# All attention exponentials through the DMA transpose: one transpose path instead of two, with three score buffers

## The chip, the cores and the metric

The kernel runs on one core of one Trainium2 chip. The metric is the device time of one execution in microseconds (us), the median of several runs. Five engines work side by side, each through its own queue in order: TensorE (PE; its weight loads are shown apart as PEld), VectorE (DVE), ScalarE (ACT), GpSimd (POOL) and SyncE (SP), which here only issues DMAs.

## The reference

The input x has 4 batches of 1024 tokens with 256 features. Four residual layers follow one another, each on a layer norm of x: a linear recurrence (LRU) with a small MLP, a gated feed-forward with two top-32 selections per token (FFN), an attention, and the same FFN again. The change touches the attention alone, but the attention runs beside parts of both FFNs.

```python
q = (x @ Wq.T).reshape(b, t, N_HEADS, HEAD_DIM)          # 8 heads of 64
kv_latent = x @ Wkv_down.T                               # 64 wide, shared by the heads
k = (kv_latent @ Wk_up.T).reshape(b, t, N_HEADS, HEAD_DIM)
v = (kv_latent @ Wv_up.T).reshape(b, t, N_HEADS, HEAD_DIM)
scores = jnp.einsum('bqhd,bkhd->bhqk', q, k) * scale
attn = jax.nn.softmax(scores, axis=-1)                   # no mask: 1024 keys for each query
out = jnp.einsum('bhqk,bkhd->bqhd', attn, v)
return out.reshape(b, t, N_HEADS * HEAD_DIM) @ Wo.T
```

Wk_up is folded into the queries and Wv_up into the output weights, so that keys and values of all heads are the same 64-wide latent rows. kh and kl are its two parts with the tokens along the free axis; la (float32), or lb0 and lb1 (float16 high and low part), are the same rows with tokens on the partitions.

## The kernel before

The work is in stages. The LRU and the first layer norm of the FFN come first; then the first FFN's tiles of batch 0 with the attention's preparation; then, with pools of their own, the attention of all four batches; then the rest of the second FFN. The middle stage is the one that changes. In it heads() runs for each batch b over 2 blocks of 512 queries (nb), 4 pairs of heads (g) and 4 tiles of 128 queries (q): 32 iterations a batch, 128 in all. An iteration treats two heads (j = 0, 1), called halves here: 256 halves in all. A half is a chain over the engines: PE multiplies queries by keys into a PSUM tile sc of 128x1024 (line 877), DVE takes the negated maximum of each row (nm, 881), ACT takes the exponential into pr and sums the rows (885). For the product with the values the exponentials must lie with the keys on the partitions, so they are transposed. There are two ways, and by_dma picks by the parity of q:

- q even: ACT casts pr to float16 (888), POOL forms the remainder as a second float16 (889), both into pd; SP issues one DMA that transposes all of it into d0 or d1 (890). DVE has added 11 ln 2 to the maximum's negative before (883), so that the small parts stay in range. The values are then summed over 24 terms per half, in float16 (values_sum, line 921).
- q odd: PE transposes pr itself, eight blocks per half into PSUM tiles ptp of four (896); ACT copies them out to p0 or p1 (901; in the last batch DVE copies every first one, 899). The values are summed over 8 terms per half, in float32.

values_sum also takes the reciprocal of the row sums (rs, 915), spreads it on POOL (rows, 917), lets PE transpose that (929), copies it (rb, ACT, 931) and multiplies (on, DVE, 932). It is called late: for an odd q in the next iteration's first half, for an even q in the second half of the next even iteration, so that the DMA has time to land.

merge() weaves side work into the halves at fixed places: the queries of the next group (queries, 849), the output product of a finished query block (output, 942 and 944), the second FFN's layer norm and first product on finished tokens (head), the next batch's keys (prepare, values), and for b < 3 the eight FFN tiles of the next batch (tile: two top-32 selections on DVE at line 670, with POOL, ACT and PE parts; it starts at half 12 + 4i of 64). The order that results on each engine is then set by a scheduler with a timeline of its own; each engine follows that order.

PSUM has eight banks. In this stage two score buffers take four ("sc": 2), the transposes two ("t": 2) and all else shares two ("s": 2). In SBUF, d0 and d1 have two buffers each, pd two, pr three, rows two, xg (the tile's gated input, line 651) two.

Of the kernel before, what the change touches and what calls it, by code (L numbers as in the profile page):

```python
# [10 lines left out]
F32 = mybir.dt.float32  # L11
# [3 lines left out]
F16 = mybir.dt.float16  # L15
AF = mybir.ActivationFunctionType
ALU = mybir.AluOpType
AX = mybir.AxisListType
PSUM = bass.MemoryType.PSUM
DRAM = bass.MemoryType.DRAM  # L20

P = 128
B = 4
T = 1024
D = 256
KD = D // P
TPB = T // P
# [3 lines left out]
HD = 64  # L31
# [455 lines left out]
class Ffn:  # L487
# [100 lines left out]
    def tile(self, i, sp, psum, tags, out=None, fast=False, parts=None, tt=None):  # L588

        nc, w = self.nc, self.w  # L590
# [14 lines left out]
        nm = sp.tile([P, 2], F32, tag="nm", name="nm")  # L605
        ssum = sp.tile([P, 2], F32, tag="ssum", name="ssum")
# [11 lines left out]
        for r in range(nr):  # L618
            for s in range(2 if r else 0):
                self.ordered(nc.vector.max, m8[:, s, r, :], wk[:, s, :])  # L620
            for s in range(2):
                v, k = (wk, m8[:, s, r, :]) if r else (ex, e8[:, s, :])
# [6 lines left out]
        q = i % 4  # L629
# [17 lines left out]
            pool.tensor_tensor(ob, ob, ex[:, 0, :], ALU.mult)  # L647
        yield

        xg = sp.tile([P, D], F32, tag="xg", name="xg", bufs=2)  # L650
        sc = sp.tile([P, 2], F32, tag="sc", name="sc")
        pool.tensor_scalar(sc, norm[:, :, q], rs[:, 1:2], 0.0, ALU.mult, ALU.add)
        nc.scalar.activation(xg, x, AF.Identity, bias=sc[:, 1:2], scale=sc[:, 0:1])
# [112 lines left out]
PSHIFT = 11  # L766


class Attention:
# [8 lines left out]
    def prepare(self, b, nb, psum, tag, groups=((0, 1), (2, 3)), whole=True):  # L778


        nc, sp, wp = self.nc, self.sp, self.wp
        xs = self.x[b * TPB + 4 * nb : b * TPB + 4 * nb + 4]
        xnt = self.xnt[b, nb] = [
            wp.tile([P, KD, 512], F32R, tag=f"xnt{nb}{part}", name=f"xnt{nb}{part}") for part in range(2)
        ]
        if nb == 0:
            self.k[b] = (
                wp.tile([P, T], F32R, tag="kh", name="kh", bufs=2),
                wp.tile([P, T], F32R, tag="kl", name="kl", bufs=2),
                wp.tile([P, TPB, HD], F32, tag="la", name="la", bufs=2),  # L790
                [wp.tile([P, TPB, HD], F16, tag=f"lb{i}", name=f"lb{i}", bufs=2) for i in range(2)],
            )
        if whole:
            scales = layer_norm(nc, sp, "ax4", xs)
            yield
        for group in groups:
            views = [xs[q] for q in group]
            if whole:
                rstd, shift = (t[:, group[0] : group[-1] + 1] for t in scales)
            else:  # L800
                rstd, shift = layer_norm(nc, sp, f"ax{len(group)}", views)
                yield
            pt = normalized_t(nc, sp, psum, "fx", tag, views, rstd, shift, self.ident)
            sl = slice(group[0] * P, (group[-1] + 1) * P)
            split(nc, *(t[:, :, sl] for t in xnt), pt)
            if not whole:
                self.latents(b, nb, sl, psum, tag)
            yield
        if whole:
            self.latents(b, nb, slice(0, 512), psum, tag)  # L810
            yield
# [11 lines left out]

    def values(self, b, nb, psum, tag):

        nc, (kh, kl, la, lb) = self.nc, self.k[b]
        pv = psum.tile([P, 4, HD], tag, "pv")
        for q in range(4):
            tk = slice((4 * nb + q) * P, (4 * nb + q + 1) * P)
            for i, v in enumerate((kh, kl)):  # L830
                nc.tensor.matmul(pv[:, q, :], v[0:HD, tk], self.sident, start=(i == 0), stop=(i == 1))
        sl = slice(4 * nb, 4 * nb + 4)
        nc.scalar.copy(la[:, sl, :], pv)
        nc.gpsimd.tensor_copy(lb[0][:, sl, :], la[:, sl, :])
        nc.gpsimd.tensor_tensor(lb[1][:, sl, :], la[:, sl, :], lb[0][:, sl, :], ALU.subtract)
        yield

    def queries(self, b, nb, g, psum, tag):
# [13 lines left out]
    def heads(self, b, psum):  # L852

        nc, sp, wp = self.nc, self.sp, self.hp
        kh, kl, la, lb = self.k[b]
        late, pending = [], []
        for nb, g, q in ((nb, g, q) for nb in range(2) for g in range(PAIRS) for q in range(4)):
            by_dma = q % 2 == 0  # L860
            if g == 0:
                self.on[b, nb, q] = wp.tile([P, PAIRS, P], F32, tag=f"on{q}", name=f"on{q}")
            qs = self.qs[b, nb, g]
            ssum = sp.tile([P, 2], F32, tag="ssum", name="ssum", bufs=4)
            if by_dma:
                pts = [wp.tile([P, 2 * TPB, P], F16, tag=f"d{j}", name=f"d{j}", bufs=2) for j in range(2)]
                parts = ((0, lb[0]), (TPB, lb[0]), (0, lb[1]))
                terms = [(v[:, c, :], i + c) for c in range(TPB) for i, v in parts]
            else:
                pts = [wp.tile([P, TPB, P], F32, tag=f"p{j}", name=f"p{j}") for j in range(2)]  # L870
                terms = [(la[:, c, :], c) for c in range(TPB)]
            for j in range(2):
                sc = psum.tile([P, T], "sc", "sc")
                for i, kk in enumerate((kh, kl)):
                    for kb in range(2):
                        sl = slice(kb * 512, (kb + 1) * 512)
                        nc.tensor.matmul(  # L877
                            sc[:, sl], qs[:, j, q * P : (q + 1) * P], kk[:, sl], start=(i == 0), stop=(i == 1)
                        )
                nm = sp.tile([P, 1], F32, tag="nm", name="nm", bufs=4)  # L880
                nc.vector.tensor_reduce(nm, sc, AX.X, ALU.max, negate=True)  # L881
                if by_dma:
                    nc.vector.tensor_scalar(nm, nm, PSHIFT * math.log(2.0), None, ALU.add)  # L883
                pr = wp.tile([P, T], F32, tag="pr", name="pr", bufs=3)
                nc.scalar.activation(pr, sc, AF.Exp, bias=nm, accum_out=ssum[:, j : j + 1])  # L885
                if by_dma:
                    pd = wp.tile([P, 2, T], F16, tag="pd", name="pd", bufs=2)
                    nc.scalar.copy(pd[:, 0, :], pr)  # L888
                    nc.gpsimd.tensor_tensor(pd[:, 1, :], pr, pd[:, 0, :], ALU.subtract)  # L889
                    nc.sync.dma_start_transpose(pts[j], pd.rearrange("p i k -> p (i k)"))  # L890
                else:
                    for half in range(2):
                        pt = psum.tile([P, 4, P], "t", "ptp")
                        for kk in range(4):
                            kc = 4 * half + kk
                            nc.tensor.transpose(pt[:, kk, :], pr[:, kc * P : (kc + 1) * P], self.ident)  # L896
                        dst = pts[j][:, 4 * half : 4 * half + 4, :]
                        if half == 0 and b == B - 1:
                            nc.vector.tensor_copy(dst, pt)
                        else:  # L900
                            nc.scalar.copy(dst, pt)  # L901
                if j == 0 and pending:
                    self.values_sum(*pending.pop(0), psum)
                if j == 1 and late and by_dma:
                    self.values_sum(*late.pop(0), psum)
                yield
            (late if by_dma else pending).append((pts, terms, ssum, self.on[b, nb, q][:, g, :]))
        for args in late + pending:
            self.values_sum(*args, psum)

    def values_sum(self, pts, terms, ssum, on, psum):

        nc, sp = self.nc, self.sp
        rs = sp.tile([P, 2], F32, tag="rs", name="rs")
        nc.vector.reciprocal(rs, ssum)
        rows = sp.tile([P, 2, HD], F32, tag="rows", name="rows")
        nc.gpsimd.tensor_copy(rows, rs[:, :, None].to_broadcast([P, 2, HD]))  # L917
        po = psum.tile([P, 2, P], "s", "pmo")
        for n, (v, c) in enumerate(terms):
            for j in range(2):  # L920
                nc.tensor.matmul(  # L921
                    po[j * HD : (j + 1) * HD, 0, :],
                    v,
                    pts[j][:, c, :],
                    start=(n == 0),
                    stop=(n == len(terms) - 1),
                )

        nc.tensor.transpose(po[:, 1, :], rows.rearrange("p j d -> p (j d)"), self.ident)  # L929
        rb = sp.tile([P, P], F32, tag="rb", name="rb", bufs=1)  # L930
        nc.scalar.copy(rb, po[:, 1, :])  # L931
        nc.vector.tensor_tensor(on, po[:, 0, :], rb, ALU.mult)  # L932
# [92 lines left out]
def tile_kernel(ctx: ExitStack, tc: tile.TileContext, x_in, w_lru, vecs_in, rows, w_ffn, lin_t, w_attn, w_down, out):  # L1025
    nc = tc.nc
# [33 lines left out]
    with ExitStack() as c1:  # L1060
# [16 lines left out]
        for k in range(NBLK):  # L1077
# [11 lines left out]
            b = k // CH + 1  # L1089
# [10 lines left out]
        k = NBLK - 1  # L1100
# [13 lines left out]
    with ExitStack() as c2:  # L1114
# [8 lines left out]
        with ExitStack() as c4:  # L1123
# [8 lines left out]
            with tc.issue_after(f1.gelu(1)):  # L1132
                for blk in range(2, NBLK):
                    g = f1.gelu(blk)
# [26 lines left out]
                    next(aheads, None)  # L1161
            run(second)
            f1.keep, f1.last_topk = False, None
        psum = Banks(c2.enter_context(tc.tile_pool(name="ps2", space=PSUM)), {"sc": 2, "t": 2, "s": 2})
        at.hp = c2.enter_context(tc.tile_pool(name="at_h", bufs=1))
        fp = c2.enter_context(tc.tile_pool(name="f_s", bufs=2))
        for b in range(B):
# [130 lines left out]
```

## Time and profile before

| | us |
|---|---|
| median of 3 runs | 1562.88 |
| lowest and highest | 1562.34, 1567.57 |
| the profiled execution, its own time | 1561.58 |
| its span in the trace | 1559.9 |
| of that, up to the first scores of the attention | 376.7 |
| the attention stage, 376.7 to 1335 | 958.3 |
| what follows | 224.9 |

The profile shows one execution. Busy time of an engine is the time in which it works on an instruction; a wait is idle time in front of an instruction, with the instruction that ended it. Times of POOL are rough, and ends of matmuls are modelled. In the tables of stretches each row gives, for each engine, busy microseconds and in brackets the instructions; then the granted PE clock (1.00 is full), the mean share of the 16 DMA engines that was busy (a share over 1 means that packets stood one behind the other), and GB/s.

### The profile page before, as it was taken

The numbers are of one execution on the slowest core, as the hardware profiler recorded it, in microseconds if no ns is written. First come the engines' busy times: TensorE is split into PE (matmuls) and PEld (weight loads), VectorE is DVE, ScalarE is ACT, GpSimd is POOL, SyncE is SP. The second block draws the span as 40 slices with busy tenths as digits, with TensorE's granted clock in tenths as the row PEclk, the third lists the DMA queues.
The fourth block names the chain that finished last, engine by engine and source line by source line (L and its number), as shares of the span: only waits on it lengthen the run. The fifth ranks groups of instructions, "written<-read, shape, count | busy, mean of one in ns | idle before, by whom it ended". The sixth has DMA issues, their size and how long they took to land.

```text
span 1559.9 us, 28683 instructions
## 1 busy us (share of the span) xinstructions
PE 1303.3 (84%) x10136; PEld 955.5 (61%) x10136; DVE 1193.4 (77%) x3674; ACT 1014.4 (65%) x2145; POOL 681.7 (44%) x848
## 2 busy tenths in 40 slices
PE   5879999697898789988879988879989998667776
PEld 3535556375766667756657866657777776444544
DVE  8977675696599966778976568986675665499998
ACT  5253434654787668777677877767875875476664
POOL 2043423161365533536543435643443533157876
PEclk9989999698999999999999999999999999779888
DMA  3110000331544334453334443414443545000000
GB/s 116 35 36 14 28 14 17 130 122 34 82 79 89 58 62 82 82 86 68 59 61 83 82 72 75 85 35 82 83 82 56 99 79 82 14 11 28 21 24 28
DMA packets 288609, 96.51 MB, mean 62 GB/s; under 512 B 268233, under 2 KB 284626, under 8 KB 288466
## 3 DMA queue, kind: packets, MB, share of 16 engines
q1 hardware_dynamic: 283024, 88.50, 29.3%
q10 hardware_dynamic: 5442, 6.18, 1.2%
q8 instruction: 80, 1.31, 0.3%
q14 instruction: 63, 0.52, 0.1%
HBM read 16.01 MB, written 11.53 MB: 18 GB/s over the span
## 4 chain that ended last, share of the span: by engine, by line
DVE 40%; PE 35%; ACT 12%; DMA 5%; issue 5%; POOL 2%; SPq 0%; ACTq 0%; POOLq 0%; DVEq 0%
DVE wk L670 9%; PE pmo L921 8%; DVE nm L881 7%; DVE m L670 7%; PE sc L877 6%; DMA d<-pd 4%; ACT pr L885 4%; PE po L436 2%; PE ptp L896 2%; PE pmy L170 2%; DVE qs L849 2%; PE pu L170 2%; PE pz L451 1%; ACT p L901 1%; PE pmo L929 1%
## 5 line engine op out<-in xcount | busy, mean ns | idle before, releaser
L889 POOL TENSOR_TENSOR pd<-pr,pd 128x1024 f16<-128x1024 f32 x128 | 274.1, 2145 | 256.0 <-ACT pd L888 173.5
L881 DVE TENSOR_REDUCE nm<-sc 128x1 f32<-128x1024 f32 x256 | 310.2, 1216 | 74.1 <-PE sc L877 72.8
L885 ACT ACTIVATE pr<-sc,nm 128x1024 f32<-128x1024 f32 x256 | 286.9, 1122 | 112.1 <-DVE nm L883 63.3
L877 PE MATMUL sc<-kh,qs 128*128 128x512 f32 x512 | 183.6, 439 | 30.9 <-ACT pr L885 22.6
L877 PE MATMUL sc<-kl,qs 128*128 128x512 f32 x512 | 161.6, 397 | 0.0
L896 PE MATMUL ptp<-ident,pr 128*128 128x128 f32 x1024 | 143.6, 278 | 16.9 <-ACT pr L885 12.1
L670 DVE MATCH_REPLACE8 wk<-m,wk 128x256 f32<-128x256 f32 x384 | 155.4, 408 | 0.3
L888 ACT CAST pd<-pr 128x1024 f16<-128x1024 f32 x128 | 134.1, 1050 | 32.8 <-DMA d<-pd 31.4
L921 PE MATMUL pmo<-p,la 128*64 128x128 f32 x2048 | 139.5, 284 | 12.8 <-DVE xnt L161 6.0
L670 DVE MAX8 m<-wk 128x8 f32<-128x256 f32 x384 | 149.9, 413 | 0.1
L901 ACT COPY p<-ptp 128x512 f32<-128x512 f32 x224 | 125.4, 592 | 27.9 <-PE ptp L896 18.7
L921 PEld LDWEIGHTS pmo<-p,la 128*64 128x64 f32 x2048 | 118.8, 141 | 38.4 <-issue 15.2
L896 PEld LDWEIGHTS ptp<-ident,pr 128*128 128x128 f32 x1024 | 117.4, 142 | 40.0 <-ACT pr L885 17.9
L877 PEld LDWEIGHTS sc<-kh,qs 128*128 128x128 f32 x512 | 83.0, 194 | 60.6 <-ACT pr L885 42.6
L624 POOL TENSOR_TENSOR ex<-ex,wk 128x512 f32<-128x512 f32 x61 | 77.9, 1276 | 92.3 <-DVE wk L670 73.0
L921 PE MATMUL pmo<-d,lb 128*64 128x128 f16 x3072 | 103.2, 223 | 12.5 <-DMA d<-pd 3.6
L877 PEld LDWEIGHTS sc<-kl,qs 128*128 128x128 f32 x512 | 96.8, 190 | 22.3
L921 PEld LDWEIGHTS <-lb 128*64 128x64 f16 x3072 | 92.5, 111 | 28.4 <-issue 24.5
L695 PE MATMUL pf<-wf,vt 128*128 128x256 f32 x288 | 86.1, 441 | 4.9 <-ACT vt L693 4.3
L917 POOL COPY rows<-rs 128x128 f32<-128x128 f32 x128 | 36.9, 294 | 115.7 <-PE pmo L929 85.9
L932 DVE TENSOR_TENSOR on<-pmo,rb 128x128 f32<-128x128 f32 x128 | 36.3, 284 | 62.0 <-ACT rb L931 61.2
L147 PE MATMUL pt<-ident,xn 128*128 128x128 f32 x256 | 47.9, 306 | 38.2 <-ACT xn L145 29.6
(306 smaller groups left out, 2791.0 us busy)
## 6 DMA issues: line engine op xcount, KB each, us to landing
tt<-ft SPq DMA_DIRECT2D x16, 256.0 KB
tt<-tt SPq DMA_DIRECT2D x8, 512.0 KB
out<-x SPq DMA_DIRECT2D x32, 128.0 KB
x<-in_x ACTq DMA_DIRECT2D x6, 512.0 KB
pf<-pfs SPq DMA_DIRECT2D x12, 256.0 KB
full<-pf SPq DMA_DIRECT2D x24, 128.0 KB
d<-pd SPq DMA_TRANSPOSE x128
wa<-in_w_attn SPq DMA_DIRECT2D x2, 640.0 KB
```

The lines of the kernel that those rows point to most:

```text
L170: nc.tensor.matmul(dst, x, y, start=start and i == 0, stop=stop and i == len(terms) - 1)
L624: pool.tensor_tensor(ex, ex, wk, ALU.subtract)
L670: ins = make(*args).ins
L695: nc.tensor.matmul(dst, vt[:, k, :], w.wf[:, k, :], start=(k == 0 and bias is None), stop=(k == KD - 1))
L877: nc.tensor.matmul(sc[:, sl], qs[:, j, q * P : (q + 1) * P], kk[:, sl], start=(i == 0), stop=(i == 1))
L881: nc.vector.tensor_reduce(nm, sc, AX.X, ALU.max, negate=True)
L885: nc.scalar.activation(pr, sc, AF.Exp, bias=nm, accum_out=ssum[:, j : j + 1])
L888: nc.scalar.copy(pd[:, 0, :], pr)
L889: nc.gpsimd.tensor_tensor(pd[:, 1, :], pr, pd[:, 0, :], ALU.subtract)
L896: nc.tensor.transpose(pt[:, kk, :], pr[:, kc * P : (kc + 1) * P], self.ident)
L901: nc.scalar.copy(dst, pt)
L921: nc.tensor.matmul(po[j * HD : (j + 1) * HD, 0, :], v, pts[j][:, c, :], start=(n == 0), stop=(n == len(terms) - 1),)
```

## The change

All 128 iterations take the DMA way; the PE transposes, their PSUM banks, p0, p1 and the float32 values in the products are gone. The two freed PSUM banks become a third score buffer. d0 and d1 get a third buffer and pd has four. To make room, la becomes a short-lived tile in the tag of the layer norm's xn, and xg and rows go from two buffers to one. values_sum of an iteration is called two iterations later, in the second half.

```diff
-        xg = sp.tile([P, D], F32, tag="xg", name="xg", bufs=2)
+        xg = sp.tile([P, D], F32, tag="xg", name="xg", bufs=1 if parts else 2)
...
+        la = self.sp.tile([P, D], F32, tag="fx_xn", name="la", bufs=2).rearrange("p (q d) -> p q d", q=4)
+        nc.scalar.copy(la, pv)
...
-        late, pending = [], []
+        pending = []
         for nb, g, q in ((nb, g, q) for nb in range(2) for g in range(PAIRS) for q in range(4)):
-            by_dma = q % 2 == 0
...
+            pts = [wp.tile([P, 2 * TPB, P], F16, tag=f"d{j}", name=f"d{j}", bufs=3) for j in range(2)]
+            parts = ((0, lb[0]), (TPB, lb[0]), (0, lb[1]))
+            terms = [(v[:, c, :], i + c) for c in range(TPB) for i, v in parts]
             ssum = sp.tile([P, 2], F32, tag="ssum", name="ssum", bufs=4)
-            if by_dma:
...
-            else:
-                pts = [wp.tile([P, TPB, P], F32, tag=f"p{j}", name=f"p{j}") for j in range(2)]
-                terms = [(la[:, c, :], c) for c in range(TPB)]
...
-                if by_dma:
-                    nc.vector.tensor_scalar(nm, nm, PSHIFT * math.log(2.0), None, ALU.add)
+                nc.vector.tensor_scalar(nm, nm, PSHIFT * math.log(2.0), None, ALU.add)
...
-                if by_dma:
-                    pd = wp.tile([P, 2, T], F16, tag="pd", name="pd", bufs=2)
...
-                else:
-                    for half in range(2):
-                        pt = psum.tile([P, 4, P], "t", "ptp")
-                        for kk in range(4):
-                            kc = 4 * half + kk
-                            nc.tensor.transpose(pt[:, kk, :], pr[:, kc * P : (kc + 1) * P], self.ident)
...
-                if j == 0 and pending:
+                pd = wp.tile([P, 2, T], F16, tag="pd", name="pd", bufs=4)
+                nc.scalar.copy(pd[:, 0, :], pr)
+                nc.gpsimd.tensor_tensor(pd[:, 1, :], pr, pd[:, 0, :], ALU.subtract)
+                nc.sync.dma_start_transpose(pts[j], pd.rearrange("p i k -> p (i k)"))
+                if len(pending) > 1 and j == 1:
                     self.values_sum(*pending.pop(0), psum)
-                if j == 1 and late and by_dma:
-                    self.values_sum(*late.pop(0), psum)
...
-        rows = sp.tile([P, 2, HD], F32, tag="rows", name="rows")
+        rows = sp.tile([P, 2, HD], F32, tag="rows", name="rows", bufs=1)
...
-        psum = Banks(c2.enter_context(tc.tile_pool(name="ps2", space=PSUM)), {"sc": 2, "t": 2, "s": 2})
+        psum = Banks(c2.enter_context(tc.tile_pool(name="ps2", space=PSUM)), {"sc": 3, "s": 2})
```

More of the change, by code (lines that the diff above doesn't have):

```diff
@@ L789, in prepare @@
                 wp.tile([P, T], F32R, tag="kl", name="kl", bufs=2),
-                wp.tile([P, TPB, HD], F32, tag="la", name="la", bufs=2),
                 [wp.tile([P, TPB, HD], F16, tag=f"lb{i}", name=f"lb{i}", bufs=2) for i in range(2)],
@@ L824, in values @@
     def values(self, b, nb, psum, tag):
-        nc, (kh, kl, la, lb) = self.nc, self.k[b]
+        nc, (kh, kl, lb) = self.nc, self.k[b]
         pv = psum.tile([P, 4, HD], tag, "pv")
@@ L831, in values @@
                 nc.tensor.matmul(pv[:, q, :], v[0:HD, tk], self.sident, start=(i == 0), stop=(i == 1))
+        la = self.sp.tile([P, D], F32, tag="fx_xn", name="la", bufs=2).rearrange("p (q d) -> p q d", q=4)
+        nc.scalar.copy(la, pv)
         sl = slice(4 * nb, 4 * nb + 4)
-        nc.scalar.copy(la[:, sl, :], pv)
-        nc.gpsimd.tensor_copy(lb[0][:, sl, :], la[:, sl, :])
-        nc.gpsimd.tensor_tensor(lb[1][:, sl, :], la[:, sl, :], lb[0][:, sl, :], ALU.subtract)
+        nc.gpsimd.tensor_copy(lb[0][:, sl, :], la)
+        nc.gpsimd.tensor_tensor(lb[1][:, sl, :], la, lb[0][:, sl, :], ALU.subtract)
         yield
@@ L856, in heads @@
         nc, sp, wp = self.nc, self.sp, self.hp
-        kh, kl, la, lb = self.k[b]
-        late, pending = [], []
+        kh, kl, lb = self.k[b]
+        pending = []
         for nb, g, q in ((nb, g, q) for nb in range(2) for g in range(PAIRS) for q in range(4)):
-            by_dma = q % 2 == 0
             if g == 0:
@@ L863, in heads @@
             qs = self.qs[b, nb, g]
+            pts = [wp.tile([P, 2 * TPB, P], F16, tag=f"d{j}", name=f"d{j}", bufs=3) for j in range(2)]
+            parts = ((0, lb[0]), (TPB, lb[0]), (0, lb[1]))
+            terms = [(v[:, c, :], i + c) for c in range(TPB) for i, v in parts]
             ssum = sp.tile([P, 2], F32, tag="ssum", name="ssum", bufs=4)
-            if by_dma:
-                pts = [wp.tile([P, 2 * TPB, P], F16, tag=f"d{j}", name=f"d{j}", bufs=2) for j in range(2)]
-                parts = ((0, lb[0]), (TPB, lb[0]), (0, lb[1]))
-                terms = [(v[:, c, :], i + c) for c in range(TPB) for i, v in parts]
-            else:
-                pts = [wp.tile([P, TPB, P], F32, tag=f"p{j}", name=f"p{j}") for j in range(2)]
-                terms = [(la[:, c, :], c) for c in range(TPB)]
             for j in range(2):
@@ L881, in heads @@
                 nc.vector.tensor_reduce(nm, sc, AX.X, ALU.max, negate=True)
-                if by_dma:
-                    nc.vector.tensor_scalar(nm, nm, PSHIFT * math.log(2.0), None, ALU.add)
+                nc.vector.tensor_scalar(nm, nm, PSHIFT * math.log(2.0), None, ALU.add)
                 pr = wp.tile([P, T], F32, tag="pr", name="pr", bufs=3)
                 nc.scalar.activation(pr, sc, AF.Exp, bias=nm, accum_out=ssum[:, j : j + 1])
-                if by_dma:
-                    pd = wp.tile([P, 2, T], F16, tag="pd", name="pd", bufs=2)
-                    nc.scalar.copy(pd[:, 0, :], pr)
-                    nc.gpsimd.tensor_tensor(pd[:, 1, :], pr, pd[:, 0, :], ALU.subtract)
-                    nc.sync.dma_start_transpose(pts[j], pd.rearrange("p i k -> p (i k)"))
-                else:
-                    for half in range(2):
-                        pt = psum.tile([P, 4, P], "t", "ptp")
-                        for kk in range(4):
-                            kc = 4 * half + kk
[L896 to L901, printed above, removed]
-                if j == 0 and pending:
+                pd = wp.tile([P, 2, T], F16, tag="pd", name="pd", bufs=4)
[3 more added lines that the diff above has]
+                if len(pending) > 1 and j == 1:
                     self.values_sum(*pending.pop(0), psum)
-                if j == 1 and late and by_dma:
-                    self.values_sum(*late.pop(0), psum)
                 yield
-            (late if by_dma else pending).append((pts, terms, ssum, self.on[b, nb, q][:, g, :]))
-        for args in late + pending:
+            pending.append((pts, terms, ssum, self.on[b, nb, q][:, g, :]))
+        for args in pending:
             self.values_sum(*args, psum)
```

## The prediction

> **What bounds the kernel now.** I read the page's busy shares first: PE works 84% of the span, but that mixes stages. So I cut the attention stage (376.7 to 1335 us, 958.3 us, 256 halves, 3.74 us a half) out with the table by stretches, in pieces of 16 halves:
>
> ```profile
> 376.70:1335.00 958.30, 839.36 (x8367) 658.67 (x8369) 703.82 (x1727) 705.52 (x1374) 429.05 (x420) 0.98 0.43 74
> 420.00:500.00 80.00, 71.95 (x702) 55.15 (x701) 73.98 (x219) 65.60 (x143) 46.16 (x51) 1.00 0.52 91
> 604.40:654.20 49.80, 48.45 (x520) 40.20 (x521) 29.18 (x56) 41.37 (x76) 25.29 (x22) 1.00 0.44 68
> ...
> 718.40:775.40 57.00, 49.11 (x441) 37.78 (x437) 52.03 (x154) 44.39 (x96) 33.76 (x35) 1.00 0.44 74
> 775.40:852.90 77.50, 64.97 (x647) 50.38 (x643) 57.38 (x149) 55.34 (x108) 26.90 (x29) 0.96 0.39 73
> ```
>
> There are two kinds of pieces. Seven have no selections on DVE (604.4 is one); there PE is 97% busy and is the bound. I call them light: together 376 us with PE 346, ACT 274, DVE 224, POOL 162. Nine carry the next batch's FFN tiles (718.4 is one); there DVE is 91% busy and PE close behind. I call them heavy: 582 us with PE 493, DVE 480, ACT 431, POOL 267. Then the groups of the stage (busy us, mean ns, idle before them) give the prices:
>
> ```profile
> L881 DVE TENSOR_REDUCE nm<-sc 128x1 f32<-128x1024 f32 x256 | 310.2, 1216 | 74.1 <-PE sc L877 72.8
> L889 POOL TENSOR_TENSOR pd<-pr,pd 128x1024 f16<-128x1024 f32 x128 | 274.1, 2145 | 256.0 <-ACT pd L888 173.5 <-issue 25.6 <-DVE ax_v L55 18.8
> L896 PE MATMUL ptp<-ident,pr 128*128 128x128 f32 x1024 | 143.6, 278 | 16.9 <-ACT pr L885 12.1 <-ACT p L901 4.6
> L921 PE MATMUL pmo<-p,la 128*64 128x128 f32 x2034 | 138.7, 284 | 12.8 <-DVE xnt L161 6.0 <-DVE qs L849 4.9 <-ACT ft L523 0.7
> L888 ACT CAST pd<-pr 128x1024 f16<-128x1024 f32 x128 | 134.1, 1050 | 32.8 <-DMA d<-pd 31.4
> L901 ACT COPY p<-ptp 128x512 f32<-128x512 f32 x224 | 125.4, 592 | 27.9 <-PE ptp L896 18.7 <-PE pmo L921 8.7
> L921 PE MATMUL pmo<-d,lb 128*64 128x128 f16 x3072 | 103.2, 223 | 12.5 <-DMA d<-pd 3.6 <-DVE x L944 3.0 <-DVE on L932 2.5
> L883 DVE TENSOR_SCALAR nm<-nm 128x1 f32<-128x1 f32 x128 | 18.7, 146 | 1.5
> ```
>
> The busy column divided by the count is the price that an operation adds to its engine (34 ns for a float16 value product); the mean is longer where operations overlap. Last, two views of what is shared: two transposes one behind the other, us by us, and two DVE operations.
>
> ```profile
> 915.00:916.00 1.00, 1.00 (x7) 0.80 (x6) 0.01 (x1) 0.97 (x3) 0.00 (x0) 1.00 1.15 214
> ...
> 918.00:919.00 1.00, 0.88 (x6) 0.84 (x7) 0.42 (x3) 0.46 (x1) 0.00 (x0) 1.00 1.17 217
> ```
> ```profile
> L64 DVE SCALAR_TENSOR_TENSOR fx_t<-norm_f x21: 132/163/2061, 530.1 to 1256.8; 128x4 f32<-128x4 f32 x21
> L632 DVE SCALAR_TENSOR_TENSOR full<-full,rs,ex x24: 474/607/1976, 435.4 to 1056.9; 128x256 f32<-128x256 f32 x24
> ```
>
> A transpose moves 128x2048 float16, 524 KB; at about 213 GB/s that is 2.5 us during which the DMA engines are full, so two of them do not overlap. And a DVE operation of four columns takes 0.16 us as a rule but once 2.06, as long as one POOL subtraction.
>
> **The change, part by part** (sums for the whole stage).
> PE loses the transposes and the float32 products, 143.6 + 138.7, and gains as many float16 products, 103.2: -179, to 660 us; light 268, heavy 393.
> ACT gains 128 casts, 134.1, and loses 224 copies, 125.4: +9, to 714. In the last batch, where half of the copies lay on DVE, it gains more: light 286, heavy 421.
> POOL gains 128 subtractions: +274, to 703; light 282, heavy 422.
> DVE gains 128 small adds, 18.7, and loses the 32 copies of the last batch, 21.9 (their row): -3. An add sits between maximum and exponential in every half, so it lengthens the chain by 0.15 us too.
> DMA: 256 transposes by 2.5 to 2.6 us are 640 to 666 us; the other loads of the stage (24 of 128 KB) add 15. SP issues 256 of them at about 2 us each (the median of its rows), 510 us of a queue with nothing else but these loads behind it. A late transpose holds back only later ones.
>
> So five resources come to lie near 700 where one was at 839. If all were interchangeable in time, the stage could fall to 740; it can't, because the selections stay where the halves put them.
>
> Heavy pieces: DVE is now alone at the top: 480 + 10 for the adds, and the lock. DVE operations with two SBUF inputs (117 in the layer norms' root and ten or so beside it, 24 in L632) already stand about 38 us over their shortest time, summed from means minus usual durations in their rows. POOL's busy share of the stage rises from 0.45 to about 0.77 and that of the 2.1 us instruction more than doubles, so I take 38 to 70, of which 30 more fall here: 520 us. Against this stands a rule. The Trainium skill (SBUF — State Buffer, section "Who interferes with whom") says that a DVE instruction with two SBUF inputs and a GpSimd instruction that reads SBUF exclude each other for the whole instruction. If all 150 met a full subtraction, that would be 150 x 2.1 = 315 us instead of 70 and the change would lose. The row shows a median of 0.16, so most meet none; I keep the row, scaled, and leave the rule's end to a rival. The best DVE stretch in this trace has 73.98 of 80 us, 92%. With no PE near it and a third score buffer against the 72.8 us that DVE waited for scores, I take 92%: 520 / 0.92 = 566 us, 16 less.
>
> Light pieces: ACT 286, POOL 282, DMA 291 (112 halves by 2.6) are equal, and every half passes all three. One engine alone reached 97%; the whole stage, with a clear leader, 839 / 958 = 88%. Three equal ones get a little less, 86%: 291 / 0.86 = 338, 38 less.
>
> Ends: now the last iteration goes over PE. Behind the last exponential there will be cast, subtraction, transpose (about 1.2 us to its first packet, 2.6 to its last) and products; some of this was there as PE transposes and copies: +6. A less busy PE may be granted less clock: after 1340 us PE is 67% busy and the clock 0.83. On the 2.5 us of PE work in a half's chain, 10% is 0.25 us, mostly covered by the buffers: +5, between 0 and 60.
>
> Small edits: xg with one buffer is cost at nothing. Tiles start four halves apart, some 14 us, and PE has read xg long before; without that cover it would be 24 waits of some 2 us on ACT (a wait for px ahead of vt is about 2.8). la as a passing tile is the same copy. Ahead of rows POOL idles already 86 us for PE to release it, with two buffers; with one I take the same 86, as values now come later, ends 40 and 230; it is inside the 86%.
>
> Sum: -16 - 38 + 6 + 5 = -43 on the profiled execution's 1561.6, so 1519; the median is 1.3 above that execution: 1520.
>
> **Rivals.**
> *More gain* (0.12): the two added buffers let the selections spread, heavy pieces at 96% (542) and light ones at 93% (313). That gives -40 - 63 + 5: about 1465. Against it: each engine's order is fixed beforehand.
> *No change* (0.12): a loop through the buffers. In the changed program's PE order the values of an iteration stand behind the scores of 6 to 14 later halves; 29 of 128 stand 12 or more back. Such a score waits for an exponential, that for a subtraction (pr), that for a cast, and that for a transpose (pd) only three halves ahead of the one that these values must release (d). The loop is cast 1.05, subtraction 2.14, exponential 1.3, scores 1, values 1.5, transpose 3.8: 10.8 us and hand-offs. At 11.6 us for three halves it is 3.9 a half, no more than the heavy pieces take anyhow. If queueing makes it 14, those 58 halves cost 0.7 us more each, 41 us, and the gain is gone: 1561. In favour: SP already waits 350 us for values before transposes.
> *Slower* (0.33): POOL holds the lock when DVE wants it. The place is DVE's selection pieces. If POOL's subtractions stand in a row, a root's ten operations each meet one. At a mean wait of 1.07 us, half a subtraction, 150 operations cost 160 us instead of 38: heavy DVE is 612, at 92% 665, +83, and with the light pieces' -38 and the +11 it is 1618. It decides from a mean wait of about 0.7 us (now 0.25). That POOL also idles ahead of rows makes its backlog likelier. Against it: POOL would have to be late all the time, and DVE's maximum, most of its work, reads PSUM and is always 1.2 us.
> That the change does not do what it says is excluded: SP's order has 256 transposes.
>
> **How the numbers follow.** The case of the sum has 0.43, its own range 1490 to 1550; more gain 0.12; no change 0.12; slower 0.33. A measurement of this kernel can tell 0.5%, about 8 us, from no change. Faster 0.55, same 0.12, slower 0.33. The range, 1455 to 1600, takes in the larger gain and most of the slower case, but not its full price.
>
> **What would show it.** Right: a stage of about 915 us; light pieces near 3.0 us a half and heavy ones near 3.9; PE busy near 660 with idle time, POOL 700, ACT 715; transposes of 2.6 us nearly back to back in light pieces; L632 and the root's operations with means of 0.5 us more at most. Wrong: light pieces that do not get shorter (then rows, pd or the loop hold POOL or ACT); heavy pieces over 4.2 us a half with DVE busy over 600 (the lock) or with DVE idle on scores (the loop); PE's clock well under 0.9.

## The result and the profile after

The changed kernel takes 1640.1 us (median of 4 runs, 1636.0 to 1642.0) against 1562.6 for the kernel before in the same comparison: ratio 1.0491, 95% interval 1.0454 to 1.0528, so 77 us slower. The forecast was 43 us faster, and the range ended at 1600.

The page's busy line after:

```profile
PE 1241.8 (76%) x10136; PEld 883.9 (54%) x10136; DVE 1200.9 (73%) x3770; ACT 1031.4 (63%) x2049; POOL 947.4 (58%) x976
```

No engine is busier than 76% of the span, and POOL has gained its 266 us. The table by stretches shows where the time is (before the stage, the stage from the first maximum to the last attention output, the rest; the same cut of the kernel before stands under it):

```profile
0.00:379.50 379.50, 312.12 (x1207) 197.93 (x1208) 287.46 (x1094) 176.04 (x365) 114.30 (x210) 0.92 0.16 55
379.50:1415.50 1036.00, 777.42 (x8378) 587.20 (x8377) 714.42 (x1832) 722.33 (x1279) 695.88 (x549) 0.88 0.76 134
1415.50:1640.20 224.70, 152.29 (x552) 98.77 (x552) 199.05 (x846) 133.05 (x405) 137.24 (x217) 0.82 0.06 20
```
```profile
378.90:1337.70 958.80, 838.45 (x8378) 657.78 (x8377) 706.25 (x1735) 706.15 (x1375) 430.31 (x421) 0.98 0.43 74
```

All of it is in the stage: 959 to 1036 us. ACT and POOL are within 8 us of the forecast's 714 and 703; DVE, at 714, stays below the forecast's 740. PE is at 777 instead of 660. The granted clock fell from 0.98 to 0.88, which would make some 735 of the 660 (an estimate, by the ratio of the two); the other 42 us are not explained here. But all engines now wait, the busiest a quarter of the time. The DMA share is 0.76.

To compare like with like I cut both traces at the same halves (each 16th maximum of scores, line 881 before, 875 after). A light piece (halves 64 to 79), a heavy one (96 to 111) and the one behind it (112 to 127), before and after:

```profile
616.40:667.30 50.90, 48.04 (x517) 39.45 (x516) 33.66 (x67) 40.15 (x73) 24.42 (x21) 1.00 0.50 82
729.70:804.60 74.90, 60.30 (x528) 46.46 (x528) 66.73 (x205) 52.69 (x111) 36.95 (x39) 0.95 0.34 58
804.60:864.80 60.20, 56.23 (x594) 44.17 (x589) 38.96 (x78) 47.04 (x88) 23.97 (x24) 1.00 0.42 78
```
```profile
630.90:692.10 61.20, 48.27 (x570) 38.25 (x570) 31.94 (x80) 43.61 (x72) 42.82 (x32) 0.86 0.84 142
750.50:836.90 86.40, 61.77 (x599) 47.63 (x601) 79.59 (x227) 55.72 (x110) 55.21 (x50) 0.86 0.54 104
836.90:905.00 68.10, 52.47 (x579) 38.80 (x576) 40.10 (x92) 45.12 (x77) 37.61 (x31) 0.92 0.79 130
```

The light piece did not get shorter but 10 us longer, with its busiest engine (PE) at 79% and a DMA share of 0.84. In the heavy one DVE has 13 us more work, as more of the selections fell into it, and is 92% busy. The one behind it has no engine over 77%. Summed over the stage the nine heavy pieces went from 581 to 642 us, the seven light ones from 378 to 394.

What do the engines wait for? In SP's queue the sums of the values lead, as they did before (us in total, times, longest):

```profile
SPq L890 <- PE pmo L921: 349.7, 45, 21.3
```
```profile
SPq L882 <- PE pmo L900: 299.1, 61, 17.4
```

The first line is before, the second after. In the waits of the stage ACT's cast has grown, before and after:

```profile
POOL pd L889 <- ACT pd L888: 173.5, 56, 12.8
ACT pd L888 <- DMA d<-pd: 31.4, 17, 5.1
```
```profile
POOL pd L881 <- ACT pd L880: 165.9, 107, 15.0
ACT pd L880 <- DMA d<-pd: 139.3, 118, 3.5
```

Read backwards, this is the loop of the prediction's rival: a transpose waits up to 17 us for a value sum to free its d buffer, the casts wait for the transpose to free pd (139 us instead of 31), and POOL, behind them, idles. POOL's wait itself is no longer than before. The loop ran at half the transposes before, covered there in part by PE's work (e7 shows below that it was not covered in full); now every half goes through it.

### The profile page after: what moved, and what is told of

The parts are those of the page before. It is cut to its first block, busy times and chain, and to the rows that moved or that the text cites. A ratio compares the mean times of both kernels' runs of the same rounds, so it can differ in the third digit from the quotient of the medians.

```text
span 1640.2 us, 29253 instructions
## 1 busy us (share of the span) xinstructions
PE 1241.8 (76%) x10136; PEld 883.9 (54%) x10136; DVE 1200.9 (73%) x3770; ACT 1031.4 (63%) x2049; POOL 947.4 (58%) x976
## 4 chain that ended last, share of the span: by engine, by line
DVE 31%; PE 25%; DMA 14%; ACT 11%; issue 10%; POOL 9%; SPq 0%; ACTq 0%; POOLq 0%; DVEq 0%
DMA d<-pd 13%; DVE wk L670 7%; DVE m L670 5%; DVE nm L875 5%; POOL pd L881 5%; PE sc L871 4%; ACT pd L880 3%; PE pmo L900 3%; ACT pr L878 3%; PE po L436 3%; PE pmy L170 2%; PE pu L170 2%; PE pz L451 1%; PE pf L695 1%; PE pl L555 1%
## 5 line engine op out<-in xcount | busy, mean ns | idle before, releaser
L881 POOL TENSOR_TENSOR pd<-pr,pd 128x1024 f16<-128x1024 f32 x256 | 545.4, 2138 | 174.9 <-ACT pd L880 165.9
L880 ACT CAST pd<-pr 128x1024 f16<-128x1024 f32 x256 | 267.4, 1047 | 140.9 <-DMA d<-pd 139.3
L900 PE MATMUL pmo<-d,lb 128*64 128x128 f16 x6144 | 229.8, 237 | 56.1 <-DMA d<-pd 13.6
L900 PEld LDWEIGHTS <-lb 128*64 128x64 f16 x6144 | 208.0, 121 | 99.3 <-issue 70.4
L871 PE MATMUL sc<-kh,qs 128*128 128x512 f32 x512 | 199.5, 473 | 80.5 <-ACT pr L878 49.7
L170 PE MATMUL pmy<-wvo,onp 128*128 128x256 f32 x384 | 68.9, 330 | 19.4 <-ACT onp L920 13.4
L555 PE MATMUL pl<-lint,xc_f 128*128 128x512 f32 x128 | 77.8, 698 | 5.3 <-ACT xc_f L586 5.3
L170 PEld LDWEIGHTS pmy<-wvo,onp 128*128 128x128 f32 x384 | 61.6, 230 | 31.0 <-ACT onp L920 16.7
L849 DVE TENSOR_TENSOR qs<-pmq,qs 64x512 fp32r<-64x512 f32 x64 | 44.0, 688 | 46.0 <-ACT qs L848 45.1
L147 PEld LDWEIGHTS pt<-ident,xn 128*128 128x128 f32 x256 | 33.4, 160 | 80.6 <-ACT xn L145 30.3
```

Source lines behind the costliest of these rows:

```text
L147: nc.tensor.transpose(pt[:, k, i * P : (i + 1) * P], xn[:, k * P : (k + 1) * P], ident)
L170: nc.tensor.matmul(dst, x, y, start=start and i == 0, stop=stop and i == len(terms) - 1)
L555: self.last_logits = nc.tensor.matmul(v, x, w.lint, start=False, stop=True).ins
L871: nc.tensor.matmul(sc[:, sl], qs[:, j, q * P : (q + 1) * P], kk[:, sl], start=(i == 0), stop=(i == 1))
L900: nc.tensor.matmul(po[j * HD : (j + 1) * HD, 0, :], v, pts[j][:, c, :], start=(n == 0), stop=(n == len(terms) - 1),)
```

## The experiments

The kernel before ran beside each variant on the same chip (1561.7 to 1563.3 us), and ratios are against it. A difference between two variants is that of their medians.

**Score buffer or shared banks (e1, e2).** The change gave both freed banks to the scores. e1 gives them to all else, e2 to nobody.

```diff
-{"sc": 3, "s": 2}
+{"sc": 2, "s": 4}    # e1
+{"sc": 2, "s": 2}    # e2
```

> The changed kernel, but the two freed PSUM banks go to the tag s, which all else shares (sc 2, s 4 instead of sc 3, s 2). Theory 1 (values late in PE's order: with two banks for everything the sums get a bank late, so a transpose waits for its d buffer and the cast behind it for pd; here the order of the built program has the values 4 to 9 halves behind their scores instead of 6 to 14): about 1480 to 1530 us, SP's wait for values falls from 299 us to under 100, ACT's wait of the cast for the DMA from 139 us to under 50. Theory 2 (POOL's lock on DVE): nothing changes, 1630 or more. Theory 3 (the slower PE clock by itself): still 1600 or more, clock near 0.88. Theory 4 (DMA time: 256 transposes of 2.6 us are too many beside the chain): about 1600.

Measured: 1570.6 us, ratio 1.0049 (1.0032 to 1.0066). SP's wait for values fell from 299 to 27 us and the casts' for the DMA from 139 to 5. So theory 1 found most of the loss, 69 us of 77, though not the gain that it expected.

> The changed kernel with the third score buffer taken away and the two banks left unused (sc 2, s 2). Theory 1: the third score buffer let PE's order put more scores ahead of the values (values now 4 to 12 halves behind, mean 7.2 instead of 10); without it the loop is looser: 1590 to 1620. If the third score buffer is what helps (the forecast's view): slower, 1660 or more. Theories 2 to 4: within 1% of 1640.

Measured: 1649.9 us, ratio 1.055 (1.0516 to 1.0584). The third score buffer is worth about 10 us, near the noise (the two intervals overlap), but on the side where the forecast had it: it is not the harm that theory 1 saw in it. The harm is in the two shared banks: from e2 to e1 it is two more of them, and 79 us.

**Buffers of the loop (e3) and length of the transposes (e4).**

```diff
-d{j} bufs=3, pd bufs=4
+d{j} bufs=4, pd bufs=2          # e3
-nc.sync.dma_start_transpose(pts[j], pd.rearrange("p i k -> p (i k)"))
+nc.sync.dma_start_transpose(pts[j], pd[:, 0, :])      # e4, and the sums read d's one half twice
```

> The changed kernel with the buffers moved: d 4 instead of 3, pd 2 instead of 4 (as in the kernel before). Theory 1: the loop through d has one iteration more of slack, but the cast is held by pd two halves earlier; values stand 6 to 12 halves behind, mean 7: 1580 to 1640. Theories 2 and 3: no change. Theory 4: slower, as fewer transposes can queue: 1660.

Measured: 1719.8 us, ratio 1.1016 (1.0968 to 1.1064). A miss in size: with pd back at two the casts waited 221 us for the DMA and SP no longer for values. The tightest link moved and got worse, so pd's four buffers carried a good part of the all-DMA kernel.

> The changed kernel with only the high float16 part transposed: each DMA moves half (262 KB); POOL still forms the remainder but it goes nowhere, and the value sums read the high part twice, so PE, ACT, DVE and POOL do the same work in an order with the same lag of the values (mean 9.5 halves instead of 10). Theory 4 (DMA time): 1500 to 1550, the transposes then take about 1.3 us each. Theory 1: the loop is shorter by 1.3 to 2.6 us of some 13: 1590 to 1620. Theories 2 and 3: within 1% of 1640.

e4 leaves the low float16 parts out of the transposes and the sums. Measured: 1618.2 us, ratio 1.035 (1.0317 to 1.0382): 22 us less, nearest to theory 1. While values come late, shorter transposes help little; SP then waits 479 us for values instead.

**Three shared banks, and the clock (e5, e6, e15).** e5 is `{"sc": 2, "s": 3}`. e6 and e15 add products into the eighth bank to keep PE busy:

```diff
+                dm = psum.tile([P, 512], "w", "dm")
+                for _ in range(3):                     # e15: once
+                    nc.tensor.matmul(dm, self.filler[0], self.filler[1], start=True, stop=True)
```

> The changed kernel with two score buffers, three banks for all else and one bank unused. Theory 1 in its present form (with two shared banks the value sums get a bank late, so they stand late in PE's order and hold d and pd): the third shared bank does most of it, values stand 4 to 9 halves behind as with four: 1560 to 1585 us (e1: 1571), SP's wait for values under 60 us. If it was the fourth bank that counted: 1610.

Measured: 1575.0 us, ratio 1.0083 (1.0062 to 1.0104): one more shared bank does nearly all of what two do.

> e5 with the unused bank as target of three bf16 products of 128x512 per half (768 in all) whose result nobody reads: extra work for PE of about 0.21 us each, 0.64 us a half, 165 us in all, to keep its granted clock up. Theory 3 (the clock, 0.88 instead of 0.94, is what e1 and e5 still lose): clock 0.95 or more and 1530 to 1560, faster than e5 in spite of the added work. Without the clock's effect: the same as e5 to 3% slower, 1570 to 1620.

> e5 with one filler product per half instead of three (256 of 0.21 us, 55 us of PE work). e6 raised the clock from 0.90 to 0.93 of the span with 165 us of added work and lost 8 us, which leaves open whether the clock gained what the work cost. If the clock counts: clock about 0.92 and 1555 to 1570. If not: 1573 to 1585.

Measured: e6 1582.8 us (ratio 1.013, 1.0111 to 1.0149), e15 1579.6 (1.0094, 1.0058 to 1.0129). Nothing ties a filler to its half, and the fillers ran ahead: e15's 256 all lie between 387 and 789 us, e6's 768 between 384 and 1201. So the stretch to look at is 380 to 790 us, here in e5, e6 and e15:

```profile
380.00:790.00 410.00, 320.83 (x3354) 238.51 (x3354) 327.00 (x884) 301.54 (x555) 295.68 (x245) 0.90 0.78 137
```
```profile
380.00:790.00 410.00, 381.61 (x3811) 256.35 (x3811) 331.47 (x903) 310.18 (x570) 301.04 (x249) 0.98 0.80 140
```
```profile
380.00:790.00 410.00, 370.43 (x3560) 245.98 (x3560) 323.60 (x865) 298.30 (x547) 291.73 (x241) 0.94 0.78 137
```

The clock rose from 0.90 to 0.98 and 0.94, and the first 128 halves took 491 us in e5, 491 in e6 and 498 in e15. The lower clock goes with the change, but these runs show no time that giving it back would return. Since the filler also takes PE's time, a gain of up to its own 55 or 165 us, less what PE's idle time hides, could be covered by it; that much stays open.

**The kernel before with one more shared bank (e7, e12, e8).** If two shared banks hold the values back, the kernel before has the same fault. It has two banks for the PE transposes; e7 takes one.

```diff
-{"sc": 2, "t": 2, "s": 2}
+{"sc": 2, "t": 1, "s": 3}
```

> The kernel before with one bank moved from the PE transposes to all else (sc 2, t 1, s 3). Its values of DMA iterations stood 9 to 12 halves behind and stand 5 to 9 now. Theory 1: SP's wait for values (350 us) falls under 100; if that wait cost the kernel before something, 1510 to 1545; if PE was its bound in spite of it, 1555 to 1570. With one bank the PE transposes wait for their copies: up to 256 x 0.3 us, 1600, if that is on PE's path.

Measured: 1525.4 us, ratio 0.9768 (0.9753 to 0.9783): 36 us faster than the kernel before, nearly the 43 that the change was forecast to give. SP's wait for values fell from 350 to 104 us, and ACT's for the transposes rose from 19 to 52: the price of the bank that was taken, and covered.

> e7 (the kernel before with sc 2, t 1, s 3; 1525 us) with three pd buffers instead of two, paid for by one buffer for rows and xg as in the change. If the cast's wait for pd costs e7 something (it was 31 us in the kernel before): 1505 to 1520. If not: 1520 to 1530; slower, up to 1540, if single rows and xg hold POOL.

Measured: 1528.6 us, ratio 0.9793 (0.9764 to 0.9822): the third pd buffer, together with one buffer for rows and xg, gives nothing. POOL's wait for PE ahead of rows grew from 59 us in e7 to 130 here, but its wait for DVE's rs there fell from 75 to 32. With the smaller ones POOL waits 168 us ahead of rows in both runs: what changed is which wait ends last, not how long POOL stands.

> The kernel before with q = 0, 1, 2 over the DMA and only q = 3 over PE, and banks sc 2, t 1, s 3. Theory 1 with the forecast's balance of engines (PE 750, ACT 710, DVE 705, POOL 566, DMA 500 us in the stage): 1490 to 1540. If the DMA way is dearer than its engine time says (a chain through POOL, SP and DMA behind ACT): 1560 to 1600.

e8 sets `by_dma = q != 3`. Measured: 1604.9 us, ratio 1.0289 (1.0254 to 1.0324). A miss: worse than half and worse than all (e5). It has the kernel before's two pd and two d buffers, and its casts wait 84 us for the DMA (221 in e3, with two pd buffers as well). Whether the buffers or the share of the DMA way made it slow, this run does not separate.

**Who needs the bank (e13, e14).** e13 and e14 leave two shared banks and give the value sums one of their own.

```diff
-        po = psum.tile([P, 2, P], "s", "pmo")
+        po = psum.tile([P, 2, P], "v", "pmo")
-{"sc": 3, "s": 2}              -{"sc": 2, "t": 2, "s": 2}
+{"sc": 2, "v": 1, "s": 2}      +{"sc": 2, "t": 1, "v": 1, "s": 2}
```

> The changed kernel with sc 2, one bank of their own for the value sums (tag v) and two for all else; the eighth bank is unused. Theory 1a (the sums are late because the two shared banks are held by the side work): one bank of their own is as good as a third shared one, 1560 to 1585 (e5: 1575), SP's wait for values under 60 us. Theory 1b (any third bank loosens the side work, whose lateness is what counts): the side work still has two, 1610 to 1640.

Measured: 1558.7 us, ratio 0.9985 (0.9937 to 1.0032): 81 us less than the change, and no different from the kernel before. In the trace's PE order the sums stand 4.0 halves behind their scores on the mean; in the change it is 9.4, in e1 4.3 and in e5 4.4. SP's waits in the stage of e13 (the same view as above, its first four lines; there is no line for PE at all):

```profile
SPq L882 <- POOL pd L881: 255.0, 98, 7.8
SPq L882 <- POOL rows L896: 179.7, 83, 6.4
SPq L882 <- POOL lb L835: 40.3, 5, 31.5
SPq L882 <- POOL nm L611: 32.2, 10, 6.7
```

SP now waits for POOL's new work, and not for a buffer to come free. So the sums come in time once the side work no longer takes their banks. The side work gains too, as it now has its two banks alone; how much of the 81 us is its share, no run separates.

> The same in the kernel before (sc 2, t 1, v 1, s 2). Theory 1a: as e7, 1520 to 1535. Theory 1b: 1550 or more. Values stand 3 to 10 halves behind in the built order.

Measured: 1525.2 us, ratio 0.9758 (0.9742 to 0.9773), as e7. So with a bank of their own for the sums in both, all over the DMA is 1558.7 and half over it 1525.2: the change of path, with its buffers, costs 33 us where the forecast saw a gain of 43. But SP still waits 208 us for the sums in e14, and they stand 7.9 halves behind (8.6 in the kernel before, 5.6 in e7):

```profile
SPq L890 <- PE pmo L921: 103.9, 24, 8.5
```
```profile
SPq L890 <- PE pmo L921: 207.9, 43, 10.9
```

The first line is e7, the second e14, and their times are the same. So in the kernel before the time does not follow this wait one to one. A bank more is worth 37 us there; whether by earlier sums or by side work that no longer shares with them stays open.

**What the DMA path costs with enough banks (e9, e10, e11).** e9 is e5 with e4's edit, so it leaves out the low parts; e10 also leaves out POOL's line; e11 has more pd and calls the values earlier.

```diff
-                nc.gpsimd.tensor_tensor(pd[:, 1, :], pr, pd[:, 0, :], ALU.subtract)     # e10
-                if len(pending) > 1 and j == 1:        # e11, with d bufs=2, pd bufs=6, s 4
+                if pending and j == 1:
```

> e5 (all over the DMA, sc 2, s 3; 1575 us) with half of each transpose left out, as in e4 (only the high part is moved, and read twice). It asks what keeps e5 50 us behind e7, the half-and-half kernel with the same shared banks (1525). If the 2.6 us of each transpose do it (DMA engines over 80% busy in e5): 1525 to 1545. If not, as for e4 in proportion: 1560 to 1575.

> e9 with POOL's subtraction left out too (256 x 2.14 us, 549 us less on POOL, and no lock on DVE from it). If POOL's queue or its lock is what is left: 1480 to 1530, and the DVE operations with two SBUF inputs return to 0.5 and 0.16 us. If neither counts: within 10 us of e9.

> All over the DMA with sc 2, s 4; the values of an iteration are called one iteration later instead of two, so that d can do with two buffers and pd gets six. If the remaining loss of e1 (1571) is the cast's wait for pd and the loop through d: 1530 to 1550. If it is the load on ACT, DVE, POOL and DMA together, nearly equal: 1560 to 1580.

Measured: e9 1533.3 us (ratio 0.9826, 0.9796 to 0.9855), 42 less than e5. e10 1484.1 (0.9504, 0.9474 to 0.9533), 49 less than e9. e11 1582.5 (1.0129, 1.0101 to 1.0157): more pd and an earlier call gain nothing once the banks are there.

So half of each transpose's time is worth 42 us, and POOL's subtraction 49. By pieces, e9 takes 29 us from the light ones and 13 from the heavy; e10 takes 43 of its 51 us of stage from the heavy ones, where DVE's selections are. There the lock shows. The view of one tile, full (L632: minimum, median, maximum ns), in e9 and in e10:

```profile
L632 DVE SCALAR_TENSOR_TENSOR full<-full,rs,ex x24: 449/1112/2437, 426.4 to 1047.3; 128x256 f32<-128x256 f32 x24
```
```profile
L632 DVE SCALAR_TENSOR_TENSOR full<-full,rs,ex x24: 467/477/1141, 428.0 to 997.1; 128x256 f32<-128x256 f32 x24
```

Without the subtractions the median falls to the minimum, and the roots' operations with it: all those rows together (lines 56, 64 to 66, 136 and 632) are 89 us in e9 and 43 in e10. That is 46 us of DVE time, about as much as the run gained (line 55's rows, 16 us in e9 and 3 in e10, come on top); but e10 also took 546 us from POOL's queue, and these two effects were not separated.

Transposes one behind the other look like this, us by us in a light piece of the change:

```profile
640.00:641.00 1.00, 1.00 (x12) 0.59 (x12) 0.47 (x3) 0.55 (x1) 1.00 (x1) 1.00 1.14 217
641.00:642.00 1.00, 1.00 (x44) 1.00 (x40) 1.00 (x1) 1.00 (x2) 1.00 (x2) 1.00 1.10 201
642.00:643.00 1.00, 0.64 (x14) 0.44 (x9) 0.32 (x3) 1.00 (x3) 1.00 (x3) 1.00 1.15 225
643.00:644.00 1.00, 0.96 (x5) 0.51 (x3) 0.11 (x1) 1.00 (x3) 1.00 (x1) 1.00 1.16 216
644.00:645.00 1.00, 0.00 (x0) 0.00 (x0) 1.00 (x1) 1.00 (x3) 1.00 (x2) 1.00 1.12 200
645.00:646.00 1.00, 0.78 (x3) 0.67 (x4) 0.47 (x3) 0.32 (x3) 1.00 (x2) 1.00 2.40 78
646.00:647.00 1.00, 0.58 (x3) 0.11 (x2) 0.55 (x1) 0.00 (x0) 1.00 (x1) 1.00 0.25 49
```

The DMA share stays over 1 for six us, then it falls to 0.25 for one. In such a stretch a half comes no faster than one transpose, 2.5 us; over the whole piece, 16 halves in 61.2 us, it is 3.8.

## Why the prediction was wrong, point by point

**Prices and sums of DVE, ACT and POOL: right.** In the stage ACT measured 722 (forecast 714), POOL 696 (703), DVE 714 (740 with the lock). The subtraction is still 2.14 us, the transposes still fill the DMA engines at some 210 GB/s. The kernel's trouble is not in any of these rows.

**The step that failed first: banks that "all else" shares were taken as unchanged.** The prediction read sc 2 to 3 as a gain and priced nothing for the tag s, since it had two banks before and after. But before, only every other iteration's values led to a transpose's buffer; now all do. The prediction saw the trace of it (SP waiting 350 us for values; sums 6 to 14 halves behind in the order) and put it under "No change" at 41 us. It measured 81 us (the change against e13, which gives up the third score buffer as well). The loop named there was right, its cause was not: it took the lateness as given and did not ask which resource made it so. e1, e5 and e13 show that it is PSUM banks: two for the sums and the side work together are too few. Each variant is scheduled anew, so a part of any one difference may be the new order; that four placements of banks (e1, e5, e13, and e7 in the other kernel) agree speaks against that being much. Of the 120 us between the forecast and the measurement these are 81; the other 39 are in the light pieces below.

**Heavy pieces: 566 forecast, 642 measured, 567 in e13, and that agreement is luck.** The term was 520 us of DVE at 92%. In e13 the nine pieces have 467 us of DVE, 82% of their 567 (the sum row of the table by stretches):

```profile
sum 566.70, PE 454.35 PEld 340.13 DVE 467.00 ACT 425.60 POOL 414.50; mean PE 50.48 PEld 37.79 DVE 51.89 ACT 47.29 POOL 46.06
```

Some selections fell into light pieces there (the first of these has 46.8 us of DVE in 58), so the work was smaller than 520, and the share was smaller than 92%. The two errors cancel. The share had been read from single pieces: in the prediction's own cut DVE's 480 us are 82% of the heavy 582, and PE, with 493, is busier than DVE. Each of the three batches with tiles has a heavy piece like that at 836.9 to 905.0 above, where DVE is at 59%.

**Light pieces: 338 forecast and 11 for the ends, 394 measured, and still 388 in e13.** This term was mis-sized, whatever the banks. The prediction let three equal resources (ACT 286, POOL 282, DMA 291) run at 86%. In e13 ACT ran at 75% (291 of 388) and POOL at 73% (283). The DMA share reads 0.86 to 1.03 in six of the seven pieces there; as it counts packets that stand behind one another, it does not tell how near the DMA was to its limit. Of the three, the runs tried two: half the DMA time took 29 us off the light pieces (e9), POOL's subtraction 8 more (e10); ACT's casts were not tried. My reading of it, which no run separates from the load itself: each transpose takes its 2.6 us after 1.2 us to its first packet, behind the one before it, so every half became a chain cast, subtraction, queue, transpose, sum of which PE had held a shorter one for every other iteration. That PE has 61 us less to do (forecast 179) gains nothing by itself where PE is not the bound.

**The lock: the rival that was given the slower side, and not the cause of the loss.** It was to decide from a mean wait of 0.7 us on. The 193 operations of lines 56, 64 to 66, 136 and 632 took 81 us before and 91 in the change; e10 gives 43 as their time without the subtractions, so the wait rose from about 37 to 48 us (38 to 53 with line 55), and the forecast's 70 was too much. The Trainium skill's rule (SBUF — State Buffer, "Who interferes with whom") agrees with single rows (a maximum of 2.4 us for 0.47) and e10 shows that it costs, but it cost the kernel before nearly as much, so it does not explain the difference. Scaling it by POOL's share of the time was wrong.

**PE's clock: 5 us forecast with 60 as the end.** The clock fell by the tenth that was priced, from 0.98 to 0.88. It goes with some 75 of the 117 us that PE lies above its forecast (the estimate above). e6 and e15 show no gain from giving it back.

**Rows and xg with one buffer: as forecast, as far as seen.** POOL's wait for PE ahead of rows was 63 us in the change, 86 before, and e12, with both single, is no slower than e7 beyond the noise. In the change they were not tried alone.

## What to carry to other kernels

Where an order of instructions is fixed ahead, a shared PSUM tag takes part in setting it: look in the queue's waits for the buffer that is freed late, and ask which bank its producer waited for. Before moving work to a path of several engines because their totals have room, check what one item needs in a row there; near-equal loads on ACT, POOL and a DMA that takes one transpose at a time left ACT at 75%, not at 86%. A share of busy time read from the best piece is not that of all pieces. And a fault found in the changed kernel may be in the one before: one bank, moved, took 2.3% off it.

## What was not expected of the hardware

PE's granted clock went from 0.98 to 0.88 in the stage as PE's busy share went from 87% to 75%, and filler products brought it to 0.98 in the stretch from 380 to 790 us (e6; 0.90 in e5) without a gain in time. And a DVE operation with one small SBUF input also stood as long as a subtraction. Six of line 56 (int32, 128x4) had a median of 1.95 us in the change where the shortest is 0.2:

```profile
L56 DVE TENSOR_SCALAR ax_rs<-ax_v x6: 197/1948/2059, 523.7 to 1158.2; 128x4 int32<-128x4 int32 x6
```

It is not int32 alone. Line 55 is float32 with one SBUF input, here in e9 and, without the subtractions, in e10:

```profile
L55 DVE TENSOR_SCALAR fx_v<-fx_mv x9: 163/1651/2001, 520.8 to 1318.5; 128x4 f32<-128x4 f32 x7, 128x2 f32<-128x2 f32 x2
```
```profile
L55 DVE TENSOR_SCALAR fx_v<-fx_mv x9: 152/170/172, 509.2 to 1269.2; 128x4 f32<-128x4 f32 x7, 128x2 f32<-128x2 f32 x2
```
